# Two cross attentions with keys in rows: four heads at a time in the quarters of TensorE's array, and the maxima as one more row of the product

## The chip, the cores and the metric

The kernel runs on one core of a Trainium2 chip. The metric is the device time of one execution in microseconds (us). Each time shown is one execution; the median of the runs is compared.

## What is computed

The program is a decoder of four blocks, each with a self attention, a cross attention and a feed-forward part (twelve sub-layers), on x of 2 x 1024 tokens with 256 features. After each sub-layer comes `x = layernorm(x + sublayer(x))`. The change concerns the cross attentions of the first two blocks. Their keys are a context of 2 x 154 rows with 192 features; there are 16 heads of 16 features. Cut to what matters:

```
q = (x @ wq + bq)   k = (ctx @ wk + bk)   v = (ctx @ wv + bv)      # heads: 16 x 16
scores = einsum('bhqd,bhkd->bhqk', q, k) / sqrt(16)
scores = clip(scores, -10000, 10000)        # second block only
attn = softmax(scores, axis=-1)
out = einsum('bhqk,bhkd->bhqd', attn, v).reshape(B, Sq, 256) @ wo + bo
```

## The kernel before

`run` (L2473) calls the twelve sub-layers in the order of `LAYERS` (L2470). `l0_xattn` (L624) and `l1_xattn` (L627, with a limit of 40000 on the unscaled scores) both call `xattn` (L637). The 2048 tokens lie as 16 tiles of 128 (`x`, tokens in the partitions). Around it stand `post_norm` (L320), which normalises all 16 tiles after the sub-layer before, and the loads of the next sub-layer's weights (`after_loads`).

`xattn` first calls `xattn_keys`: it makes the keys with features in the partitions and lays them out eight times with all heads but one masked (`kx`, on GpSimd, `masked_heads` L631), makes V with keys in the partitions, writes it to DRAM and reads it back so that the 16 x 154 pairs of head and key lie one after the other in 20 chunks of 128 rows (`vb`, L2058 to L2071). Then `start_features` (L298) transposes x, two 128x128 transposes a tile, and `features` (L308) makes the queries. All products are f32. On the page one f32 product is two MATMUL instructions, one transpose is one.

The loop over the 16 tiles has these steps for each tile:

- six products with 128 rows of contraction, two or three masked heads each (L661, 462 or 308 columns, into `pa`);
- for each of them a maximum over the keys (L667, VectorE) and a subtraction (L668, VectorE in the first of the two layers, GpSimd in the second); in the second layer a clip before it (L665, VectorE);
- two exponentials of 128x1232 (L670, ScalarE);
- 20 transposes of 128x128 (L677), and five copies out of PSUM that ScalarE (L237) and VectorE (L239) take in turn;
- 20 products of the chunks with V (L689), whose last column of each head sums the weights;
- `attend_out` (L703): the reciprocal (L697) and the division (L699), two transposes (L286), the product with wo and one with a row of ones for the bias (L244), the residual (L312) and the statistics of the norm (L353, L354).

PSUM has eight banks of 128x512 f32: four of `pa`, two of `pt`, two of `po`. No order of work is written out: each engine takes its instructions in the order in which a scheduler put them at build time, and that lets the transposes and the products of one tile stand between the products of the next.

Of the kernel before, what the change touches and what calls it, by code (L numbers as in the profile page):

```python
# [25 lines left out]
T = B * S  # L26
# [16 lines left out]
def _columns():  # L43
# [7 lines left out]
    for l in ("L0", "L1", "L2"):  # L51
        v += [(f"{l}_xattn_bq", D), (f"{l}_xattn_bk", D)]
# [19 lines left out]
def _offsets(items, width):  # L72
    off, n = {}, 0
    for name, length in items:
# [9 lines left out]
          ("later", 32), ("upto", 32), ("hmask", 8), ("desc", 8), ("slots", CAP), ("rel", 17), ("eps", 2), ("vmask", 2 * NCH), ("tok", NT), ("blk", 2 * NT + NE - 1),  # L84
# [4 lines left out]
def _constants():  # L89
# [21 lines left out]
        "vmask": vmask,  # L111
        "cos": by_tile(cos), "sin": by_tile(sin),
# [12 lines left out]
def _layout(inputs):  # L125
# [3 lines left out]
    g["L3_xattn_kn_g"] = np.tile(g["L3_xattn_kn_g"], 2)  # L129
    cols = np.zeros((128, NCOL), np.float32)  # L130
# [20 lines left out]
    for m in "qkvo":  # L151
        a[f"L0x_w{m}"] = g[f"L0_xattn_w{m}"]
        a[f"L1x_w{m}"] = g[f"L1_xattn_W{m}"]
# [30 lines left out]
class Decoder:  # L184
# [426 lines left out]
    def load_xattn(self, pre, layer):  # L611
        s = self.slot()
        w = {m: self.load(s, self.ins[f"{pre}_w{m}"], 96 if m in "kv" else 128) for m in "qkvo"}
        w["bv"] = self.rows(s, f"{layer}_xattn_bv", D)
        w["bo"] = self.rows(s, f"{layer}_xattn_bo", D)
        return w
# [20 lines left out]
    def xattn(self, w, after_loads, layer, clip):  # L637
        nc, tc = self.nc, self.tc
        after_loads()
        chunks = self.xattn_chunks()  # L640
        with ExitStack() as cx:
            dram = cx.enter_context(tc.tile_pool(name="xadram", bufs=1, space=bass.MemoryType.DRAM))
            p1 = cx.enter_context(tc.tile_pool(name="xa1", bufs=1))
            p = cx.enter_context(tc.tile_pool(name="xa", bufs=2))
            kx, vb = self.xattn_keys(w, layer, p1, p, dram)
            self.start_features()
            vz = p1.tile([128, B, H, HD + 1], F, name="vz")
            nc.gpsimd.memset(vz, 0.0)
            for b in range(B):
                nc.gpsimd.tensor_copy(vz[:, b, 0:chunks[0][1]], vb[:, b, 0, 0:chunks[0][1]])  # L650
            qT = p1.tile([128, 2, T], F, name="qT")
            self.features(qT, w["q"], AF.Identity, f"{layer}_xattn_bq")
            for i in range(NT):
                b = i // TPB
                e = p.tile([128, H, SK], F, name="e")
                mx = p.tile([128, H], F, name="mx")
                for c in range(2):
                    for h0, n in ((0, 3), (3, 3), (6, 2)):
                        ps = self.pa()
                        s3 = ps[:, :n * SK].rearrange("p (h k) -> p h k", h=n)  # L660
                        nc.tensor.matmul(s3, qT[:, c, i * 128:(i + 1) * 128], kx[:, b, c, h0:h0 + n], start=True, stop=True)  # L661
                        g = slice(c * 8 + h0, c * 8 + h0 + n)
                        sub = nc.vector
                        if clip is not None:
                            nc.vector.tensor_scalar(e[:, g], s3, clip, -clip, ALU.min, ALU.max)  # L665
                            s3, sub = e[:, g], nc.gpsimd
                        nc.vector.tensor_reduce(mx[:, g], s3, AX.X, ALU.max)  # L667
                        sub.tensor_tensor(e[:, g], s3, mx[:, g].unsqueeze(2).to_broadcast([128, n, SK]), ALU.subtract)  # L668
                    g = slice(c * 8, c * 8 + 8)
                    nc.scalar.activation(e[:, g], e[:, g], AF.Exp, scale=0.25)  # L670
                eT = p.tile([128, NCH, 128], F, name="eT")
                flat = e.rearrange("p h k -> p (h k)")
                for k0 in range(0, NCH, 4):
                    ps = self.pt()
                    for k in range(k0, k0 + 4):
                        r = chunks[k][2]
                        nc.tensor.transpose(ps[:r, (k - k0) * 128:(k - k0 + 1) * 128], flat[:, k * 128:k * 128 + r], self.ident)  # L677
                    n = 4 if chunks[k0 + 3][2] == 128 else 3
                    self.copy(eT[:, k0:k0 + n].rearrange("p k t -> p (k t)"), ps[:, :n * 128])
                    if n == 3:  # L680
                        r = chunks[k0 + 3][2]
                        nc.vector.tensor_copy(eT[:r, k0 + 3], ps[:r, 384:512])
                av = self.po()
                for k, (h0, n, r) in enumerate(chunks):
                    if k == 0:
                        dst, src = av[:, :H * 17], vz[:, b].rearrange("p h d -> p (h d)")
                    else:
                        dst, src = av[:, h0 * 17:(h0 + n) * 17], vb[:r, b, k, 0:n].rearrange("p a d -> p (a d)")
                    nc.tensor.matmul(dst, eT[:r, k], src, start=(k == 0), stop=(k == NCH - 1))  # L689
                self.attend_out(p, i, av, w["o"], w["bo"])  # L690
# [1340 lines left out]
    def xattn_chunks(self):  # L2031

# [7 lines left out]
    def xattn_keys(self, w, layer, p1, p, dram):  # L2040
# [7 lines left out]
        for b in range(B):  # L2048
# [16 lines left out]
            for c in range(2):  # L2065
                self.masked_heads(kx[:, b, c], kT[:, c, b * SK:(b + 1) * SK], SK)
# [450 lines left out]
```

## Time and profile before

| what | value |
|---|---|
| runs | 3918.94, 3889.13, 3898.75 us; median 3898.75 us |
| profiled execution | 3905.38 us, its span 3903.6 us |
| mean granted TensorE clock | 0.902 |
| first cross attention: norm begins, first score product, last statistics | 780.4, 812.1, 1032.4 us |
| second: norm begins, first score product, last statistics | 1909.1, 1933.9, 2174.5 us |

Times are read from the span's start. PE is TensorE's products and PEld its loading of weights, which runs beside them; DVE is VectorE, ACT ScalarE, POOL GpSimd. "PEclk" is the granted clock of TensorE as a share of full speed. A line of groups gives the source line, the engine, the tile written and the tiles read, their shapes, the count, the busy time and the mean of one in ns, and the idle time of that engine just before them with what ended it. For a product, "32\*128 32x512" reads: 32 rows of contraction, 128 columns of weights, 512 columns that move through. A line of windows gives the busy time (and count) of each engine in one stretch of the span, the granted clock, and what the DMA engines did.

### The profile page before, as it was taken

The numbers are of one execution on the slowest core, as the hardware profiler recorded it, in microseconds if no ns is written. First come the engines' busy times: TensorE is split into PE (matmuls) and PEld (weight loads), VectorE is DVE, ScalarE is ACT, GpSimd is POOL, SyncE is SP. The second block draws the span as 40 slices with busy tenths as digits, with TensorE's granted clock in tenths as the row PEclk, the third lists the DMA queues.
The fourth block names the chain that finished last, engine by engine and source line by source line (L and its number), as shares of the span: only waits on it lengthen the run. The fifth ranks groups of instructions, "written<-read, shape, count | busy, mean of one in ns | idle before, by whom it ended". The sixth has DMA issues, their size and how long they took to land. (4 is left out here: it accounts for less than half of the span.)

```text
span 3903.6 us, 55156 instructions
## 1 busy us (share of the span) xinstructions
PE 3382.5 (87%) x22758; PEld 2236.2 (57%) x22776; DVE 1906.1 (49%) x3855; ACT 1166.2 (30%) x2063; POOL 577.2 (15%) x674
## 2 busy tenths in 40 slices
PE   8997999899779996599999479999979477789988
PEld 3544666567669995488677245544557233443345
DVE  2466765366621116787566766400020434557741
ACT  3542345333201114322222452311112233332221
POOL 0000000010023322200233113100022432210000
PEclk9996789899779998799999689999979799899989
DMA  2235432000168882466300000300023100000000
GB/s 92 74 84 136 100 77 76 7 7 1 43 242 314 324 318 72 160 272 266 95 1 1 7 8 1 120 0 0 23 94 124 62 1 25 1 1 1 1 1 22
DMA packets 181525, 317.49 MB, mean 81 GB/s; under 512 B 68176, under 2 KB 153242, under 8 KB 172186
## 3 DMA queue, kind: packets, MB, share of 16 engines
q1 hardware_dynamic: 169866, 191.13, 15.4%
q0 software_dynamic: 11408, 122.83, 8.1%
q8 instruction: 180, 2.95, 0.3%
q14 instruction: 71, 0.58, 0.0%
HBM read 265.63 MB, written 48.28 MB: 80 GB/s over the span
## 5 line engine op out<-in xcount | busy, mean ns | idle before, releaser
L244 PEld LDWEIGHTS pa<-xgT,ew 128*128 128x128 f32 x2184 | 251.4, 193 | 2.8 <-DVE xgT L816 0.8
L244 PE MATMUL pa<-xgT,ew 128*128 128x128 f32 x2184 | 251.7, 276 | 0.4 <-DVE xgT L816 0.4
L244 PE MATMUL pa<-xT,w 128*128 128x512 f32 (+3 forms) x480 | 228.1, 618 | 0.7 <-DVE xT L239 0.7
L244 PE MATMUL pa<-ha,w 128*128 128x512 f32 x512 | 220.4, 592 | 0.0
L834 DVE TENSOR_TENSOR hid<-a,pa 128x512 f32<-128x512 f32 x78 | 48.5, 621 | 294.2 <-ACT a L833 254.1
L661 PE MATMUL pa<-kx,qT 128*128 128x462 f32 (+1 forms) x384 | 174.8, 573 | 0.9 <-DVE e L668 0.5
L244 PEld LDWEIGHTS pa<-ha,w 128*128 128x128 f32 x512 | 97.3, 190 | 122.5 <-issue 122.5
L960 PE MATMUL pa<-win_k,cst 128*128 128x272 f32 x512 | 128.7, 402 | 43.5 <-DVE win_k L957 43.5
L689 PEld LDWEIGHTS po<-vb,eT 128*128 128x128 f32 (+1 forms) x1216 | 154.8, 197 | 20.3 <-issue 15.1
L689 PE MATMUL po<-vb,eT 128*128 128x34 f32 (+2 forms) x1216 | 151.9, 274 | 0.0
L237 ACT COPY eT<-pt 128x512 f32<-128x512 f32 (+2 forms) x127 | 67.5, 531 | 276.9 <-PE pt L677 221.5
L2455 DVE COPY lg<-po 128x8 f32<-128x8 f32 x16 | 2.7, 167 | 301.9 <-PE po L2452 301.9
L286 PE MATMUL pt<-cst,x 128*128 128x128 f32 x288 | 60.6, 317 | 99.4 <-DVE x L320 66.1
L244 PE MATMUL po<-w,h 128*128 128x256 f32 (+1 forms) x640 | 144.4, 382 | 0.0
L244 PEld LDWEIGHTS pa<-xT,w 128*128 128x128 f32 (+2 forms) x480 | 85.5, 189 | 98.5 <-issue 92.4
L960 PEld LDWEIGHTS pa<-win_k,cst 128*128 128x128 f32 x512 | 98.7, 195 | 63.4 <-issue 38.5
L244 PEld LDWEIGHTS po<-w,h 128*128 128x128 f32 (+1 forms) x640 | 113.2, 179 | 30.6 <-issue 8.5
L244 PE MATMUL po<-ew,hid 128*128 128x256 f32 x546 | 125.3, 379 | 0.0
L986 PE MATMUL po<-win_v,cst 128*128 128x256 f32 x544 | 120.0, 379 | 0.0
L244 PE MATMUL pa<-w,xT 128*128 128x256 f32 (+2 forms) x640 | 102.7, 323 | 15.1 <-ACT sq L1535 3.5
L833 ACT ACTIVATE a<-pa 128x512 f32<-128x512 f32 x78 | 42.4, 544 | 241.7 <-PE pa L244 241.7
L286 PEld LDWEIGHTS pt<-cst,x 128*128 128x128 f32 x288 | 38.6, 159 | 129.1 <-issue 49.9
(557 smaller groups left out, 7074.9 us busy)
## 6 DMA issues: line engine op xcount, KB each, us to landing
win_k<-kd SPq DMA_DIRECT2D x16, 2176.0 KB
win_v<-vd SPq DMA_DIRECT2D x16, 2176.0 KB
w<-in_L2f_eW_dram SPq DMA_DIRECT2D x16, 1024.0 KB
pk<-pk SPq DMA_DIRECT2D x96, 128.0 KB
rw<-pk SPq DMA_DIRECT2D x64, 128.0 KB
y<-yd SPq DMA_DIRECT2D x16, 512.0 KB
ld<-lgs SPq DMA_DIRECT2D x64, 64.0 KB
li<-ld SPq DMA_DIRECT2D x16, 256.0 KB
```

Source lines behind the costliest of these rows:

```text
L237: self.nc.scalar.copy(dst, src)
L244: self.nc.tensor.matmul(out, l, r, start=(i == 0), stop=(i == n - 1))
L286: self.nc.tensor.transpose(ps[:, c * 128:(c + 1) * 128], src[:, c * 128:(c + 1) * 128], self.ident)
L661: nc.tensor.matmul(s3, qT[:, c, i * 128:(i + 1) * 128], kx[:, b, c, h0:h0 + n], start=True, stop=True)
L689: nc.tensor.matmul(dst, eT[:r, k], src, start=(k == 0), stop=(k == NCH - 1))
L833: nc.scalar.activation(a[:, :n], pa[:, :n], AF.Silu)
L834: nc.vector.tensor_tensor(hid[:, m0:m1_].rearrange("p m t -> p (m t)"), a[:, :n], pg[:, :n], ALU.mult)
L960: nc.tensor.matmul(ps[:, 0:W * H], self.ident, win[:, :, d * H:(d + 1) * H], start=(d == 0), stop=(d == HD - 1))
L986: nc.tensor.matmul(ps[:, 0:D], self.ident, win[:, k], start=(k == 0), stop=(k == W - 1))
L2455: self.nc.vector.tensor_copy(lg[:, g * 4 + k], ps[:, :NE])
```

## The change

Both layers get a new loop; nothing else of the program is changed but the layout of their weights.

- **Layout.** On the host the query and key weights and biases are padded so that each head takes 32 feature rows: 16 with data, 16 with zeros (`wide`). Queries and keys have 512 rows, four groups G of four heads, each head in one quarter of the array's rows. Row 16 of each head holds 1 in the keys (`kb`) and a shift in the queries. V has 32 columns a head, the upper 16 of them ones, which sum the weights.
- **Scores with keys in rows.** For four tiles (512 tokens) at once, a group of four heads and 77 keys, four products in the four quarters give 77x512 scores each, in two double banks of PSUM (L737). Two exponentials of 77x1024 read them (and in the second layer two clips on VectorE follow). The products with V take the exponentials as they lie, in the four quarters of the columns (L815), so the 20 transposes a tile, their copies and V's way through DRAM fall away.
- **Maxima.** The maxima over keys are found beforehand from products with tokens in rows: eight jobs for four tiles (`find_maxima`, L710), each of eight quarter products of 154 columns into two double banks, and two reductions of 128x616. They are negated (`negate`), transposed (`shift`, four transposes) and added to the queries, where they become row 16.
- **The rest of a tile** is `divide` (four transposes, reciprocal, division), `features` (four transposes for two tiles, a copy) and `output` (two products of two passes each for a tile, residual and statistics). The output bias is added to x on GpSimd.
- **Order.** There are four groups g of four tiles. Eight steps a group are written out, and TensorE's instructions keep that order (`in_order`): the score products of the next step, one job of maxima for the group after, one piece of the group before (`pieces`), the products with V, the copy (odd steps) or the shift of the next four heads (even steps), a second job in steps 0, 3 and 6, and one piece of `prepare` for the group after the next. Group 0's queries and maxima come ahead of the loop, the last group's pieces behind it.
- **PSUM.** `wide_banks` makes one `pa`, three double banks `wide` and one `po`. Scores and jobs take turns in the three double banks; in the loop every small step (a piece, a shift, a piece of prepare) goes through the one `pa`. Ahead of the loop these steps rotate over `pa` and the double banks (`any_bank`).

The diff, with the removed body of the loop (printed above) and of `xattn_keys` left out:

```diff
-    for l in ("L0", "L1", "L2"):
-        v += [(f"{l}_xattn_bq", D), (f"{l}_xattn_bk", D)]
+    for l in ("L0", "L1"):
+        v += [(f"{l}_xattn_bq", 2 * D), (f"{l}_xattn_bk", 2 * D)]
+    v += [("L2_xattn_bq", D), ("L2_xattn_bk", D)]
...
+        "extra": p % 32 == HD,
...
+    wide = lambda t: np.pad(t.reshape(*t.shape[:-1], H, HD), [(0, 0)] * t.ndim + [(0, HD)]).reshape(*t.shape[:-1], 2 * D)
+    for l in ("L0", "L1"):
+        for m in "qk":
+            g[f"{l}_xattn_b{m}"] = wide(g[f"{l}_xattn_b{m}"])
...
-        a[f"L0x_w{m}"] = g[f"L0_xattn_w{m}"]
-        a[f"L1x_w{m}"] = g[f"L1_xattn_W{m}"]
+        as_is = wide if m in "qk" else (lambda t: t)
+        a[f"L0x_w{m}"] = as_is(g[f"L0_xattn_w{m}"])
+        a[f"L1x_w{m}"] = as_is(g[f"L1_xattn_W{m}"])
...
-        w["bo"] = self.rows(s, f"{layer}_xattn_bo", D)
+        w["bo"] = self.rows_all(s, f"{layer}_xattn_bo", D)
...
     def xattn(self, w, after_loads, layer, clip):
         nc, tc = self.nc, self.tc
         after_loads()
+        self.wide_banks()
+        since = len(nc.cur_bb.bb.instructions)
         with ExitStack() as cx:
             p1 = cx.enter_context(tc.tile_pool(name="xa1", bufs=1))
             p = cx.enter_context(tc.tile_pool(name="xa", bufs=2))
+            kp = p1.tile([128, 4, B * SK], F, name="kp")
+            vp = p1.tile([KH, B, 2, H, 2 * HD], F, name="vp")
+            pad = p1.tile([128, 4, 4, 4, 2 * HD], F, name="pad")
+            kb = p1.tile([128, 4], F, name="kb")
+            nc.gpsimd.memset(vp, 1.0)
+            nc.gpsimd.memset(pad, 0.0)
+            o = COLS[f"{layer}_xattn_bk"]
+            nc.vector.tensor_tensor(kb, self.cols[:, o:o + 4], self.k("extra").to_broadcast([128, 4]), ALU.add)
+            self.bank = self.any_bank
+            for G in range(4):
+                ps = self.bank()
+                self.mm(ps[:, :B * SK], [(w["k"][:96, c, G * 128:G * 128 + 128], self.ctxT[:96, c]) for c in range(2)])
+                nc.scalar.activation(kp[:, G], ps[:, :B * SK], AF.Identity, bias=kb[:, G:G + 1])
+            groups = NT // 4
+            fed = self.fed
+            tiles, maxima, ready = {}, {}, {}
+            def turned(src):
+                ps = self.bank()
+                for c in range(2):
+                    for t in range(2):
+                        nc.tensor.transpose(ps[:, c * 256 + t * 128:c * 256 + t * 128 + 128], src[:, t, c * 128:c * 128 + 128], self.ident)
+                return ps.rearrange("p (c t) -> p c t", c=2)
+            def prepare(g):
+                for t in range(g * 4, g * 4 + 4, 2):
+                    if not fed:
+                        self.copy(self.xT[:, :, t * 128:t * 128 + 256], turned(self.x[:, t:t + 2]))
+                        yield True
+                    for i in (t, t + 1):
+                        nc.gpsimd.tensor_tensor(self.x[:, i], self.x[:, i], w["bo"], ALU.add)
+                q = tiles[g] = p.tile([128, 4, 512], F, name="q", bufs=3)
+                for G in range(4):
+                    ps = self.bank()
+                    self.mm(ps, [(w["q"][:, c, G * 128:G * 128 + 128], self.xT[:, c, g * 512:g * 512 + 512]) for c in range(2)])
+                    nc.scalar.activation(q[:, G], ps, AF.Identity, bias=self.col(f"{layer}_xattn_bq", G))
+                    yield True
+            def find_maxima(g):
+                m = maxima[g] = p.tile([128, 4, 4, 4], F, name="m16")
+                b = g * 4 // TPB
+                for t in range(4):
+                    for G0 in range(0, 4, 2):
+                        pair = [self.wide() for _ in range(2)]
+                        for G in (G0, G0 + 1):
+                            for j in range(4):
+                                R = slice(32 * j, 32 * j + 32)
+                                o = j % 2 * 512 + (G - G0) * SK
+                                nc.tensor.matmul(pair[j // 2][:, o:o + SK], tiles[g][R, G, t * 128:t * 128 + 128],
+                                                 kp[R, G, b * SK:b * SK + SK], start=True, stop=True)
+                        for k in range(2):
+                            s = pair[k].rearrange("p (j n) -> p j n", j=2)[:, :, 0:2 * SK].rearrange("p j (G k) -> p j G k", G=2)
+                            nc.vector.tensor_reduce(m[:, t, 2 * k:2 * k + 2, G0:G0 + 2], s, AX.X, ALU.max)
+                        yield True
+            def negate(g):
+                m = maxima.pop(g)
+                if clip is not None:
+                    nc.vector.tensor_scalar(m, m, clip, 240.0 - clip, ALU.min, ALU.max)
+                for j in range(4):
+                    nc.vector.tensor_scalar(pad[:, :, :, j, HD], m[:, :, j], -1.0, None, ALU.mult)
+            def shift(g, G):
+                ps = self.bank()
+                for t in range(4):
+                    nc.tensor.transpose(ps[:, t * 128:t * 128 + 128], pad[:, t, G].rearrange("p j d -> p (j d)"), self.ident)
+                nc.vector.tensor_tensor(tiles[g][:, G], tiles[g][:, G], ps, ALU.add)
+            def scores(g, G, n):
+                b = g * 4 // TPB
+                pair = [self.wide() for _ in range(2)]
+                o = b * SK + n * KH
+                for j in range(4):
+                    R = slice(32 * j, 32 * j + 32)
+                    nc.tensor.matmul(pair[j // 2][:KH, j % 2 * 512:j % 2 * 512 + 512], kp[R, G, o:o + KH], tiles[g][R, G],
+                                     start=True, stop=True)
+                e = p.tile([KH, 4, 512], F, name="e", bufs=3)
+                for k in range(2):
+                    s = e[:, 2 * k:2 * k + 2].rearrange("p j q -> p (j q)")
+                    nc.scalar.activation(s, pair[k][:KH], AF.Exp, scale=0.25)
+                    if clip is not None:
+                        nc.vector.tensor_scalar(s, s, 1.0, float(np.exp(-60.0)), ALU.min, ALU.max)
+                return e
+            def divide(i, av, t):
+                ps = self.bank()
+                for G in range(4):
+                    nc.tensor.transpose(ps[:, G * 128:G * 128 + 128], av[:, G, t * 128:t * 128 + 128], self.ident)
+                a = ps.rearrange("p (h d) -> p h d", h=H)
+                rs = p.tile([128, H], F, name="rsum")
+                nc.vector.reciprocal(rs, a[:, :, HD])
+                if t % 2 == 0:
+                    ready[i // 2] = p.tile([128, 2, D], F, name="o")
+                nc.vector.tensor_tensor(ready[i // 2][:, t % 2].rearrange("p (h d) -> p h d", h=H), a[:, :, 0:HD],
+                                        rs.unsqueeze(2).to_broadcast([128, H, HD]), ALU.mult)
+            def features(k):
+                oT = p.tile([128, 2, 256], F, name="oT")
+                self.copy(oT, turned(ready.pop(k)))
+                ready[k] = oT
+            def output(k):
+                oT = ready.pop(k)
+                ps = self.bank()
+                for t in range(2):
+                    self.mm(ps[:, t * 256:t * 256 + 256], [(oT[:, c, t * 128:t * 128 + 128], w["o"][:, c]) for c in range(2)])
+                for t in range(2):
+                    self.residual(2 * k + t, ps[:, t * 256:t * 256 + 256])
+            def pieces(g, av):
+                i = g * 4
+                d = [lambda t=t: divide(i + t, av, t) for t in range(4)]
+                f = [lambda k=i // 2 + k: features(k) for k in range(2)]
+                u = [lambda k=i // 2 + k: output(k) for k in range(2)]
+                return [d[0], d[1], d[2], f[0], d[3], u[0], f[1], u[1]]
+            first = prepare(0)
             for b in range(B):
+                for n in range(2):
+                    next(first, None)
+                    o = b * SK + n * KH
+                    ps = self.bank()
+                    self.mm(ps[:KH, :D], [(self.ctxT[:96, c, o:o + KH], w["v"][:96, c]) for c in range(2)] + [self.row_pair(w["bv"], KH)])
+                    self.copy(vp[:, b, n, :, 0:HD], ps[:KH, :D].rearrange("p (h d) -> p h d", h=H))
+            for _ in first:
+                pass
+            ahead = prepare(1)
+            for _ in find_maxima(0):
+                next(ahead, None)
+            for _ in ahead:
+                pass
+            negate(0)
+            shift(0, 0)
+            self.bank = self.pa
+            e = scores(0, 0, 0)
+            behind = []
+            for g in range(groups):
+                b = g * 4 // TPB
+                ahead = prepare(g + 2) if g + 2 < groups else iter(())
+                jobs = find_maxima(g + 1) if g + 1 < groups else iter(())
+                av = p.tile([128, 4, 512], F, name="avs")
+                for s in range(8):
+                    G, n = divmod(s, 2)
+                    nxt = (g, *divmod(s + 1, 2)) if s < 7 else (g + 1, 0, 0)
+                    en = scores(*nxt) if nxt[0] < groups else None
+                    if s < 6:
+                        next(jobs, None)
+                    if behind:
+                        behind.pop(0)()
+                    if n == 0:
+                        ps = self.po()
+                    for j in range(4):
+                        nc.tensor.matmul(ps[32 * j:32 * j + 32], vp[:, b, n, 4 * G + j], e[:, j], start=(n == 0), stop=(n == 1))
+                    if n:
+                        nc.scalar.copy(av[:, G], ps)
+                    elif G < 3:
+                        shift(g, G + 1)
+                    if s % 3 == 0:
+                        next(jobs, None)
+                    next(ahead, None)
+                    if g + 1 < groups:
+                        if s == 5:
+                            for _ in jobs:
+                                pass
+                            negate(g + 1)
+                        if s == 6:
+                            shift(g + 1, 0)
+                    e = en
+                for f in behind:
+                    f()
+                behind = pieces(g, av)
+            for f in behind:
+                f()
+            self.in_order(since)
+        self.psum(4, 2, 2)
...
+    def wide_banks(self):
+
+        self.psum_close()
+        cx = self.psum_cx = ExitStack()
+        PS = bass.MemoryType.PSUM
+        self.psa, self.psx, self.pso = [cx.enter_context(self.tc.tile_pool(name=n, bufs=b, space=PS))
+                                        for n, b in (("psa", 1), ("psx", 3), ("pso", 1))]
+        self.pst = None
+        self.turn_bank = 0
+
+    def any_bank(self):
+
+        self.turn_bank = (self.turn_bank + 1) % 4
+        return self.wide()[:, 0:512] if self.turn_bank else self.pa()
```

## The prediction

> **What bounds the kernel now.** I read the shares of the page, then the granted clock and busy times by stage (windows), then the waits in the first layer's loop, then the products that already use parts of the array (timeline). First the page:
>
> ```profile
> PE 3382.5 (87%) x22758; PEld 2236.2 (57%) x22776; DVE 1906.1 (49%) x3855; ACT 1166.2 (30%) x2063; POOL 577.2 (15%) x674
> ...
> L661 PE MATMUL pa<-kx,qT 128*128 128x462 f32 (+1 forms) x384 | 174.8, 573 | 0.9 <-DVE e L668 0.5
> ...
> L689 PE MATMUL po<-vb,eT 128*128 128x34 f32 (+2 forms) x1216 | 151.9, 274 | 0.0
> ```
>
> The second column from the right is the idle time before: PE waits 0.9 us before 384 score products and never before 1216 products with V. By stage (length, then busy PE, PEld, DVE, ACT, POOL, granted clock, DMA):
>
> ```profile
> 779.00:812.00 33.00, 29.17 (x95) 14.95 (x96) 17.80 (x30) 9.65 (x20) 12.64 (x11) 0.90 0.20 21
> 812.00:1024.00 212.00, 210.86 (x1259) 162.44 (x1257) 148.13 (x330) 67.24 (x83) 0.00 (x0) 0.98 0.00 1
> 1024.00:1033.00 9.00, 5.85 (x25) 3.78 (x24) 2.42 (x8) 0.50 (x2) 0.00 (x0) 0.62 0.06 14
> 1905.00:1934.00 29.00, 25.45 (x83) 12.78 (x82) 10.73 (x31) 10.18 (x20) 3.33 (x8) 0.88 0.52 118
> 1934.00:2164.00 230.00, 228.29 (x1272) 172.82 (x1270) 149.26 (x330) 67.17 (x83) 83.03 (x96) 0.91 0.00 1
> 2164.00:2175.00 11.00, 5.52 (x15) 3.39 (x14) 7.12 (x13) 0.31 (x1) 0.00 (x0) 0.50 0.06 15
> 3090.00:3310.00 220.00, 163.76 (x933) 74.92 (x943) 88.88 (x257) 72.33 (x150) 73.85 (x58) 0.94 0.00 1
> 3540.00:3730.00 190.00, 179.46 (x870) 63.86 (x870) 137.87 (x168) 61.77 (x64) 0.00 (x0) 0.99 0.00 1
> ```
>
> Each layer is a start (33, 29 us), a loop (212, 230) with PE over 99% busy, and an end (9, 11). So PE's work sets the loop. The second loop is longer at the same work because its clock is 0.91. The last two rows are block 3's attentions, at a clock of 0.94 and 0.99 although PE is busy 74% and 94%. The waits of the first loop agree: everyone waits for PE.
>
> ```profile
> ACT eT L237 <- PE pt L677: 135.7, 46, 7.1
> ...
> DVE rsum L697 <- PE po L689: 17.5, 15, 1.2
> DVE eT L239 <- PE pt L677: 13.4, 30, 0.8
> ```
>
> What a set of four quarter products costs stands in block 3 (start, length):
>
> ```profile
> 3161.12 1.06 PE L1445 MATMUL po<-e,v 128*32 128x512 f32 x8
> 3162.12 1.04 PE L1432 MATMUL pa<-m_own,identb 128*128 128x512 bf16 x4
> 3163.09 1.14 PE L1436 MATMUL pa<-qT,kT 32*128 32x512 f32 x8
> 3164.16 0.44 PE L286 MATMUL pt<-cst,o 128*128 128x128 f32 x2
> ```
>
> Start to start, four column quarters take 1.00 us and four row quarters 1.07; a full product of 512 columns takes 0.86 (two instructions of 0.43). So four run nearly at once.
>
> **The change part by part.** Prices at full clock, from rows: set of row quarters 1.05, of column quarters 1.0, four transposes 0.44 (0.11 each), queries of four heads for four tiles 1.71 (four instructions of 0.43), output of two tiles 1.73 (eight of 0.216); 0.21 from the last pass to the reader's start, and about 0.1 wherever the array changes its division (1.07 against 0.96 of pure passes). Exp 77x1024 1.11 (the L2012 row), copy of 512 columns 0.59 on ACT and 0.69 on DVE, shift add 0.69, reciprocal 0.26, division 0.41, residual with statistics 1.02. A reduction of 616 is not in the trace: 308 took 0.47, 462 took 0.63, 1024 took 1.22; I take 0.78 on that line, bounds 0.63 and 1.22. The clip of 77x1024 in SBUF is bounded by 0.61 (the L1022 tensor_scalar of 2048 elements, 1.22, halved) and 1.22 (the L1611 add of 77x1024); I take 0.64, near the row of its own kind. A job's eight quarter products of 154 columns I take as 0.71 (two 64-row halves of two products took 0.40).
>
> *PE's work falls.* Before, a tile took 212/16 = 13.2 us. Now a group of four tiles takes 8 score sets 8.4, 8 V sets 8.0, 8 jobs 5.7, 48 transposes 5.2, queries 6.8, output 3.5, some 30 changes of division about 3: 40 us, against 53. Without the queries of groups 0 and 1, group 0's jobs, the shifts of its start and the last group's pieces, the loop holds 134 us.
>
> *But the order adds waits.* A typical even step (group 1, step 2, first layer), from its start: scores 0 to 1.05; exps 1.26 to 2.37 and to 3.48. The job's first two products take the third double bank at once; its third needs the first bank of the scores just issued, so it waits for the exp: 1.24 to 2.42, end 2.95. Reductions 3.16 to 3.94 and to 4.72. Divide transposes 2.95 to 3.49, but DVE has the reductions first: its reciprocal and division end at 5.39. V products end at 4.48. The shift needs the only pa bank: waits to 5.44, transposes to 5.98, add 6.19 to 6.88. The piece of prepare waits for pa again: 6.93 to 8.63. So 8.63 us for 5.5 of PE work, with waits of 1.2 (exp), 1.0 (division) and 1.0 (add). In the second layer two clips on DVE stand ahead of the reductions: the division ends 0.97 later, the step takes 9.6. An odd step without a second job (step 1) takes 6.0 and 6.9.
>
> Carried on through all steps: first layer 43.9 + 54.8 + 44.3 + 27.2 + 1 = 171 us at full clock; second 48.8 + 61.8 + 49.8 + 36.8 + 1 = 198. At a clock of 0.95 (between 0.94 and 0.99 above and the 0.91 of this layer before) PE's part stretches: 176 and 201.6. Before 212 and 230: **-36 and -28**.
>
> A page speaks against such a change: the Trainium skill, "TensorEngine Tiling (Array Packing)", section PSUM Bottleneck, says that packing speeds up TensorE but not the reading of PSUM, which may then be the limit. By that alone the loop would go by the busiest reader's sum (DVE in the second layer, about 116 us), below PE's 134, and the layer would gain; the trace's lines speak for waits by order in its place.
>
> *The start grows.* From the last product of the sub-layer before (779.1): keys 4 x 1.04, V 4 x 1.5, two turns of 0.44 and queries 4 x 1.71 = 18; the x copies on DVE wait for post_norm, which ends about 9 us in: 20. Then eight jobs beside the next group's turns and queries, all rotating over three double banks and pa: 20. Negate 0.8, shift 1.5: 42.5, at the clock of 0.90 44.8. First loop product at 823.9 instead of 812.1: **+12**. Second layer: 1905.3 + 44.8 = 1950 instead of 1933.9: **+16**. The way of V through DRAM, the masked copies (9 us on POOL) and the wider weights (loaded a stage earlier) hide in this, before and after. POOL's new memsets (0.55 for 544 elements, so about 2 each) and the additions of bo (0.82 each) lie beside DVE's norm and can slow it by a few us: bounds 0 to +4, I take 0 extra.
>
> *The end grows.* The last group's eight pieces go one after the other through pa: 16.8 us with 6 of PE. The clock fell to 0.62 and 0.50 in the ends before; at 0.6 this is 20.5. Before 8.4 (to 1032.4) and 10.5 (to 2174.5): **+12, +10**. In the second, VectorE's preparation of the next feed-forward's weights (11.8 us, which ran at the end and behind it) comes to stand between the divisions: up to +10 here, -8 behind: **+2**.
>
> The sum: +12 - 36 + 12 = -12; +16 - 28 + 10 + 2 = 0. Together -12 to -13 against the profiled execution (3905.4): 3892.8. That execution lies 6.6 above the median, so the forecast is **3886 us**.
>
> **The rivals.** *Waits shorter (faster).* If the unseen costs are at their low ends (changes of division 0.05, exp 1.02 as in the L2014 row, reduction 0.72, clip 0.61, clock 0.99), the loops take 165 and 189: -11 and -12.5, and the starts and ends together -6: about -30, 3856. For it: all stalls are in chains of such costs. If PE's work alone counted (134/0.95 = 141 us), -35 and -60 on the forecast: about 3790. Against that: the third product of each job cannot pass the exp.
>
> *The clock falls (slower).* The new loop leaves PE idle 1 us several times a step, and in the ends, where PE waited likewise, the clock was 0.62 and 0.50. At 0.75 the loops take 203 and 222 (+48 on the forecast) and starts and ends 15 more: 3949. It ends over 1% slower than before from about 0.78 down. Against it: 0.94 at 74% busy in block 3, and this loop is 78% busy.
>
> *The quarters don't run at once for 77 keys.* Four products in a row cost 3.84 instead of 1.05: 64 sets a layer +179, jobs +90: about 4420. Against it: the 32\*128 and the 128\*32 sets above.
>
> **How the numbers follow.** About 1% (39 us) is what a measurement of this kernel can tell from no change. Forecast 0.50 (its own range 3860 to 3937). Waits shorter 0.25 and PE alone 0.03: faster 0.28. Clock 0.15, quarters 0.02, and 0.05 for reductions at 1.22, clips at 1.22 and slower norms together (loops 192 and 236 at a clock of 0.9, +16 and +34, norms +8, starts and ends +6: about 3950): slower 0.22. The range reaches to the shorter waits and the lower clock and leaves out PE alone and the quarters: 3840 to 3950, with 15 us below the shorter waits because the step that PE need not wait for a bank is the least certain.
>
> **What would show it.** Right: loops of 171 to 180 and 195 to 206 us at PE busy about 78%, PE idle before the jobs' products released by ACT's exp and before shifts and prepare by DVE; starts of about 45, ends of about 20 us. Wrong: idle under 15 us in a loop (waits hidden), a granted clock under 0.85, sets of quarters over 1.3 us, or a maximum's reduction near 1.2.

## The result and the profile after

The change makes no difference that can be measured: 3909.45 us median of 20 runs against 3903.09 us of the kernel before, ratio 1.0006 with a 95% interval of 0.9985 to 1.0027. The forecast of 13 us less (0.9968) lies below that interval. The first layer gained about what was forecast; the second lost it again.

The engines' busy times fell as the change meant them to, on the page of the changed kernel:

```profile
PE 3315.3 (85%) x22774; PEld 2075.9 (53%) x22792; DVE 1814.4 (46%) x3605; ACT 1199.0 (31%) x2083; POOL 498.7 (13%) x580
...
L742 ACT ACTIVATE e<-wide 77x1024 f32<-77x1024 f32 x128 | 123.9, 1018 | 103.2 <-PE wide L737 103.2
...
L714 DVE TENSOR_REDUCE m<-wide 128x4 f32<-128x616 f32 x128 | 96.1, 792 | 87.4 <-PE wide L710 87.3
```

TensorE is busy 67 us less over the program (3382.5 before) and the time is the same. In the two loops below PE is busy 84% and 83% of the time, over 99% before, so its work alone no longer sets them. The same stages as before, from the start of the norm ahead of a layer to the first loop product, to the end of the last product with V, to the norm behind the layer (length, busy times, and the granted clock as the third number from the right):

```profile
781.43:821.70 40.27, 36.16 (x217) 19.17 (x216) 22.09 (x41) 10.92 (x17) 7.25 (x9) 0.92 0.00 1
821.70:999.10 177.40, 149.60 (x1125) 67.36 (x1125) 67.30 (x137) 78.54 (x92) 5.63 (x8) 0.94 0.00 1
999.10:1020.70 21.60, 12.94 (x44) 8.43 (x40) 7.66 (x27) 2.77 (x4) 0.00 (x0) 0.60 0.05 16
1895.12:1933.70 38.58, 34.04 (x219) 17.93 (x217) 22.35 (x42) 10.66 (x17) 6.54 (x8) 0.97 0.18 63
1933.70:2144.40 210.70, 175.26 (x1125) 78.51 (x1126) 108.87 (x204) 78.76 (x92) 5.63 (x8) 0.81 0.00 1
2144.40:2172.34 27.94, 13.50 (x44) 9.14 (x44) 18.90 (x40) 2.77 (x4) 0.00 (x0) 0.63 0.04 13
```

Read the clock: 0.94 in the first loop, 0.81 in the second. PE runs the same 1125 instructions in both, in 149.6 us and in 175.3. The stage of the first layer takes 239.3 us (252.7 before), that of the second 277.2 (269.0 before).

Why do they differ? One step with a shift and a job, first in the first layer, then in the second (start, length, and in brackets PE's idle time and who ended it):

```profile
871.57 1.32 PE L737 MATMUL wide<-q,kp 32*77 32x512 f32 x8
872.72 0.53 PE L710 MATMUL wide<-kp,q 32*128 32x154 f32 x4
874.12 0.79 PE L710 MATMUL wide<-kp,q 32*128 32x154 f32 x12 [0.86 <-ACT e L742]
874.84 0.66 PE L750 MATMUL pa<-cst,avs 128*128 128x128 f32 x4
875.43 1.07 PE L815 MATMUL po<-e,vp 77*32 77x512 f32 x8
877.00 0.63 PE L728 MATMUL pa<-cst,pad 128*128 128x128 f32 x4 [0.51 <-DVE o L756]
```

```profile
2027.67 1.10 PE L737 MATMUL wide<-q,kp 32*77 32x512 f32 x8
2028.59 0.43 PE L710 MATMUL wide<-kp,q 32*128 32x154 f32 x4
2029.88 0.79 PE L710 MATMUL wide<-kp,q 32*128 32x154 f32 x12 [0.86 <-ACT e L742]
2030.60 0.66 PE L750 MATMUL pa<-cst,avs 128*128 128x128 f32 x4
2031.18 1.06 PE L815 MATMUL po<-e,vp 77*32 77x512 f32 x8
2033.64 0.63 PE L728 MATMUL pa<-cst,pad 128*128 128x128 f32 x4 [1.39 <-DVE o L756]
2035.05 1.98 PE L252 MATMUL pa<-xT,w 128*128 128x512 f32 x4 [0.78 <-DVE q L729]
```

From its third product on the job waits 0.86 us for the exponential in both (1.2 in the prediction). The shift waits for the division 0.51 us in the first layer and 1.39 in the second (the prediction had 1.0 and 0.97 more), because VectorE has two clips (L744) ahead of the reductions and the division:

```profile
2029.86 0.69 DVE L744 TENSOR_SCALAR e<-e 77x1024 f32<-77x1024 f32 x1 [2.51 <-ACT e L742]
2030.77 0.69 DVE L744 TENSOR_SCALAR e<-e 77x1024 f32<-77x1024 f32 x1 [0.22 <-ACT e L742]
2031.38 1.49 DVE L714 TENSOR_REDUCE m<-wide 128x4 f32<-128x616 f32 x2
2032.79 0.24 DVE L753 RECIPROCAL rsum<-pa 128x16 f32<-128x16 f32 x1
2033.07 0.42 DVE L756 TENSOR_TENSOR o<-pa,rsum 128x256 f32<-128x256 f32 x1
```

So far this was in the step table. The clock was not. In the records it is at full or at half speed, in stretches of 3.41 us or multiples of it. Here are three and two neighbouring 3.41-us windows of the second loop of the changed kernel, cut on that grid (the second number is PE's busy time of the 3.41):

```profile
2044.31:2047.72 3.41, 3.41 (x23) 0.99 (x21) 0.14 (x2) 1.82 (x3) 0.00 (x0) 1.00 0.00 0
2047.72:2051.14 3.42, 1.79 (x16) 0.65 (x12) 2.50 (x4) 0.80 (x1) 0.00 (x0) 1.00 0.00 0
2051.14:2054.55 3.41, 3.41 (x11) 2.31 (x8) 1.38 (x2) 1.93 (x2) 0.00 (x0) 0.50 0.00 0
...
2071.62:2075.03 3.41, 1.49 (x12) 0.42 (x4) 2.56 (x6) 0.00 (x0) 0.00 (x0) 1.00 0.00 0
2075.03:2078.44 3.41, 2.50 (x12) 1.11 (x12) 0.19 (x1) 1.04 (x2) 0.00 (x0) 0.50 0.00 0
```

and of its first loop:

```profile
846.23:849.65 3.42, 2.50 (x32) 1.18 (x30) 0.69 (x1) 2.58 (x3) 0.00 (x0) 1.00 0.00 0
849.65:853.06 3.41, 3.41 (x32) 1.48 (x28) 2.32 (x4) 0.82 (x2) 0.00 (x0) 1.00 0.02 5
853.06:856.47 3.41, 2.49 (x32) 1.10 (x24) 0.88 (x2) 2.38 (x3) 0.00 (x0) 1.00 0.00 0
```

A window with PE busy 1.79 us (52%) or 1.49 (44%) is followed by one at half clock; the first loop's windows with 2.5 us (73%) are not. The first loop's waits mostly leave 73% or more; the second's, a little longer and close together, now and then leave half.

### The profile page after: what moved, and what is told of

Its sections match the earlier page's. It is cut to its first block, busy times and chain, and to the rows that moved or that the text cites. A ratio compares the mean times of both kernels' runs of the same rounds, so it can differ in the third digit from the quotient of the medians.

```text
span 3908.0 us, 54809 instructions
## 1 busy us (share of the span) xinstructions
PE 3315.3 (85%) x22774; PEld 2075.9 (53%) x22792; DVE 1814.4 (46%) x3605; ACT 1199.0 (31%) x2083; POOL 498.7 (13%) x580
## 3 DMA queue, kind: packets, MB, share of 16 engines
q1 hardware_dynamic: 150222, 191.05, 14.5%
## 4 chain that ended last, share of the span: by engine, by line
PE 70%; DVE 16%; ACT 5%; POOL 4%; issue 2%; DMA 2%; SPq 0%; POOLq 0%; DVEq 0%; ACTq 0%
PE pa L252 27%; PE po L252 9%; PE pa L1107 3%; PE wide L737 2%; PE po L1753 2%; PE wide L2156 2%; DVE win_v L1127 2%; PE pa L1443 1%; POOL n L1552 1%; PE wide L252 1%; PE wide L2121 1%; PE pt L294 1%; ACT e L742 1%; PE po L815 1%; PE wide L710 1%
## 5 line engine op out<-in xcount | busy, mean ns | idle before, releaser
L252 PE MATMUL pa<-xT,w 128*128 128x512 f32 (+3 forms) x488 | 237.6, 629 | 8.8 <-DVE q L729 7.5
L742 ACT ACTIVATE e<-wide 77x1024 f32<-77x1024 f32 x128 | 123.9, 1018 | 103.2 <-PE wide L737 103.2
L714 DVE TENSOR_REDUCE m<-wide 128x4 f32<-128x616 f32 x128 | 96.1, 792 | 87.4 <-PE wide L710 87.3
L294 PE MATMUL pt<-cst,x 128*128 128x128 f32 x224 | 48.7, 320 | 89.9 <-DVE x L328 65.0
L1133 PEld LDWEIGHTS po<-win_v,cst 128*128 128x128 f32 x544 | 103.4, 190 | 14.5
L252 PEld LDWEIGHTS po<-ew,hid 128*128 128x128 f32 x546 | 100.2, 190 | 11.8
L2161 ACT ACTIVATE e<-wide 128x1024 f32<-128x1024 f32 x64 | 65.6, 1025 | 129.4 <-PE wide L2156 128.7
```

Of the source, the lines that this page charges most:

```text
L252: self.nc.tensor.matmul(out, l, r, start=(i == 0), stop=(i == n - 1))
L294: self.nc.tensor.transpose(ps[:, c * 128:(c + 1) * 128], src[:, c * 128:(c + 1) * 128], self.ident)
L714: nc.vector.tensor_reduce(m[:, t, 2 * k:2 * k + 2, G0:G0 + 2], s, AX.X, ALU.max)
L742: nc.scalar.activation(s, pair[k][:KH], AF.Exp, scale=0.25)
L1133: nc.tensor.matmul(ps[:, 0:D], self.ident, win[:, k], start=(k == 0), stop=(k == W - 1))
L2161: nc.scalar.activation(e, wide, AF.Exp)
```

## The experiments

The theory under test: the clips' place on VectorE lengthens single waits of PE in the second layer until a 3.41-us window falls to about half busy, and then the clock halves. Rivals: the clock belongs to that one run; it comes from what runs before the second layer; it comes from the clips' work as such, wherever it stands. Two more edits ask what the one pa bank costs, in the loop and at the end.

Every profile gave these stages (us, granted clock of the loop in brackets):

| kernel | first: start, loop, end | second: start, loop, end |
|---|---|---|
| before | 32.1, 213.5 (0.98), 7.1 | 24.8, 230.6 (0.91), 13.6 |
| e1 before again | 32.1, 213.5 (0.98), 7.1 | 24.8, 221.1 (0.95), 13.6 |
| changed | 40.3, 177.4 (0.94), 21.6 | 38.6, 210.7 (0.81), 27.9 |
| e2 changed again | 41.9, 181.5 (0.90), 21.6 | 38.6, 214.7 (0.80), 29.1 |
| e3 only first | 42.0, 177.1 (0.94), 20.2 | 24.6, 220.5 (0.95), 13.6 |
| e4 only second | 33.3, 212.0 (0.99), 7.1 | 38.5, 214.7 (0.80), 29.2 |
| e5 no clip | 42.0, 177.2 (0.94), 20.2 | 38.6, 177.1 (0.94), 29.1 |
| e6 clip in first too | 38.1, 210.7 (0.80), 21.6 | 38.4, 209.1 (0.82), 29.2 |
| e7 late clip | 42.0, 177.1 (0.94), 20.3 | 38.5, 214.6 (0.80), 29.1 |
| e8 tail banks | 38.1, 176.8 (0.94), 12.4 | 38.5, 214.5 (0.80), 18.6 |
| e9 late clip, order kept | 42.0, 173.8 (0.97), 22.9 | 38.5, 189.9 (0.91), 29.6 |
| e10 piece first | 38.1, 163.3 (0.96), 21.7 | 38.6, 184.2 (0.90), 29.2 |
| e11 all three | 38.1, 163.8 (0.96), 13.5 | 38.6, 177.1 (0.95), 24.4 |
| e12 order kept in loop | 39.8, 160.0 (0.99), 12.4 | 38.6, 180.1 (0.93), 18.8 |

**e1 and e2, both kernels once more (no edit).**

> The kernel before, unchanged, for a second profile: how far stages that nobody changed move from one profile to another. If the clock of a stage is a matter of the run (rival), its second loop, 230 us at a granted clock of 0.91, and block 3's attention (window of 220 us at 0.94) differ by 5 us or more and by 0.03 or more of clock. If the clock belongs to the kernel (theory), both stay within 3 us and 0.02.

> The changed kernel, unchanged, for a second profile. Theory: the second layer's loop is long because TensorE's granted clock is low in it whenever this code runs: again 207 to 214 us at 0.79 to 0.84, the first layer's loop 174 to 181 us at 0.92 to 0.96. Rival (the clock was that run's): the second loop 198 to 204 us at 0.90 or more.

The old second loop in the first profile and in e1, then the new one in e2:

```profile
1933.90:2164.50 230.60, 228.89 (x1273) 173.34 (x1271) 149.26 (x330) 67.17 (x83) 83.03 (x96) 0.91 0.00 1
...
1918.10:2139.20 221.10, 219.38 (x1273) 168.01 (x1271) 148.82 (x330) 67.08 (x83) 83.03 (x96) 0.95 0.00 1
...
1936.50:2151.20 214.70, 177.72 (x1125) 78.77 (x1126) 108.91 (x204) 78.94 (x92) 5.63 (x8) 0.80 0.00 1
```

e1 and e2 are one execution each (3889.58 and 3915.96 us). The clock of the new second loop came again: 0.80, 214.7 us, just past the expected 214, and e4, e7 and e8 have it at 0.80 once more; so it belongs to the kernel. The new first loop took 181.5 us at 0.90, outside what was expected; it holds one half-clock stretch of 23.9 us that no other first loop without clips has. The old second loop moved from 230.6 us at 0.91 to 221.1 at 0.95 between two profiles, and block 3's attention by 4 us. So the run's rival holds for the old loop and falls for the new second one, and the 230 us that the prediction started from is the longest of three samples (e3 shows 220.5 once more).

**e3 and e4, one layer alone.** Edit: the other layer calls the old `xattn` with the old weights.

```diff
-        self.xattn(w, after_loads, "L1", 40000.0)
+        self.xattn_old(w, after_loads, "L1", 40000.0)     # e3; e4 the same for L0
```

> Only the first layer's cross attention is the new one, the second is as before. Theory: the first layer gains 13 us (from the start of the norm ahead of it to the norm behind it 239 instead of 253 us) and the time falls by about that, ratio 0.9967. Rival (the gain of the first layer is lost again in later stages by a lower clock): the stage gains 13 us and the time stays, ratio 0.999 to 1.001.

> Only the second layer's cross attention is the new one. Theory: its stage takes 275 to 279 us instead of 265, and the time rises by 8 to 16 us, ratio 1.002 to 1.004, with a granted clock of 0.79 to 0.84 in its loop although the first layer's old loop came before. Rival (the low clock in the second layer comes from the new first layer): loop 198 to 204 us, clock 0.9 or more, ratio 0.999 to 1.001.

e3: ratio 0.9979 (0.9952 to 1.0007), stage 239.3 instead of 252.7 us. e4: 1.0005 (0.9977 to 1.0033), stage 282.4 us with the loop at 0.80 although the old first layer ran before it. The intervals are too wide to tell 0.998 from 1; the stages are clear, though e4's is 3 us longer than the 275 to 279 expected. The new first layer is not what brings the second's clock down.

**e5, the clips left out, and e6, the clips in the first layer too.**

```diff
-                    if clip is not None:                       # e5: removed
-                        nc.vector.tensor_scalar(s, s, 1.0, float(np.exp(-60.0)), ALU.min, ALU.max)
+                    if True:                                   # e6: in both layers
+                        nc.vector.tensor_scalar(s, s, 1.0, float(np.exp(-60.0)), ALU.min, ALU.max)
```

> The changed kernel without the two clips of 77x1024 a step in the second layer (the limits of its exponentials are left out of the computation). The second loop is then the first layer's loop. Theory (the clips, ahead of the reductions and the division on VectorE, make single waits of TensorE so long that the granted clock drops): second loop 174 to 184 us at a clock of 0.90 or more, from 211 to 215 at 0.80. Of that 27 us are the waits at full clock, the rest the clock. Rival (the clock in the second layer is low because of what runs before it): clock still 0.79 to 0.84, loop 190 to 196.

> The changed kernel with the same two clips in the first layer as well (its exponentials are limited to between exp(-60) and 1, which they nearly keep anyhow). Theory: the first loop becomes like the second, 205 to 216 us at a clock of 0.78 to 0.86, from 177 to 182 at 0.90 to 0.94. Rival (the place in the program sets the clock): 198 to 203 us at 0.92 or more.

Both as the theory had it (e6 is a single execution, 3929.65 us). Without the clips the second loop is the first one, and with them the first is the second one; windows of the two loops of e5, then of e6:

```profile
809.70:986.90 177.20, 149.14 (x1125) 67.58 (x1126) 67.34 (x137) 78.30 (x92) 5.63 (x8) 0.94 0.00 1
...
1922.40:2099.50 177.10, 149.14 (x1125) 67.52 (x1126) 68.28 (x140) 78.31 (x92) 5.62 (x8) 0.94 0.00 1
```

```profile
811.50:1022.20 210.70, 176.52 (x1125) 77.98 (x1126) 107.88 (x201) 78.87 (x92) 5.62 (x8) 0.80 0.00 1
...
1956.60:2165.70 209.10, 172.88 (x1125) 76.64 (x1125) 108.70 (x204) 78.74 (x92) 5.62 (x8) 0.82 0.00 1
```

The clips add 41 us of VectorE work and 33 to 38 us to a loop of 177 us, and with them VectorE is busy only half of it. Of these 33 to 38 us, 6 to 9 are more idle time of PE (27 to 28 us without clips, 34 to 37 with them); in the rest PE's same 1125 instructions take longer (149 to 155 us without, 173 to 178 with them). e5 takes 1% less than the kernel before, 0.9901 (0.9866 to 0.9936), but it leaves the limits out.

**e7 and e9, the clips behind the reductions and the division.** e7 takes the two clips out of `scores` and issues them later; e9 also keeps VectorE's program order, as `in_order` does for PE.

```diff
+            def limit(e):
+                if clip is not None:
+                    for k in range(2):
...
                     if behind:
                         behind.pop(0)()
+                    if en is not None:
+                        limit(en)
...
             self.in_order(since)
+            self.in_order(since, mybir.EngineType.DVE)         # e9 only
```

> The clips are issued after the step's job and piece, ahead of the products with V, so that reductions and division stand before them on VectorE. The same work. Theory: second loop 188 to 194 us at a clock of 0.88 or more (186.6 at full clock by the step table), about 20 us less than with the clips ahead, ratio 0.993 to 0.998. Rival (the clock stays near 0.81): 201 to 206 us.

> As the late clip, but VectorE's instructions in the two layers now keep the program's order too, so that the clips do stand behind the job's reductions and the division. The same work, no product moved. Theory (it is the place of the clips, which makes single waits of TensorE longer, that brings the clock down): second loop 188 to 194 us at 0.88 or more; first loop 175 to 182 as before; ratio 0.993 to 0.998. Rival (the clips' work on VectorE as such, wherever it stands): 201 to 216 us at 0.79 to 0.84.

e7 is a miss: 214.6 us at 0.80, ratio 1.0035 (1.0004 to 1.0065), and in its trace the clips, reductions and reciprocals stand in the same order on VectorE as in the changed kernel, the clips ahead:

```profile
1978.85 0.69 DVE L749 TENSOR_SCALAR e<-e 77x1024 f32<-77x1024 f32 x1 [0.22 <-ACT e L742]
1979.46 1.49 DVE L714 TENSOR_REDUCE m<-wide 128x4 f32<-128x616 f32 x2
1980.87 0.24 DVE L757 RECIPROCAL rsum<-pa 128x16 f32<-128x16 f32 x1
```

VectorE's order is the scheduler's, and PE's kept order does not bind it. With the order kept (e9) the same work takes 189.9 us at 0.91, within the expected 188 to 194; ratio 0.9959 (0.9930 to 0.9989). A step of e9's second loop:

```profile
2006.96 0.79 PE L710 MATMUL wide<-kp,q 32*128 32x154 f32 x12 [0.86 <-ACT e L742]
2007.69 0.66 PE L754 MATMUL pa<-cst,avs 128*128 128x128 f32 x4
2008.28 1.07 PE L822 MATMUL po<-e,vp 77*32 77x512 f32 x8
2009.85 0.63 PE L728 MATMUL pa<-cst,pad 128*128 128x128 f32 x4 [0.51 <-DVE o L760]
```

The shift's wait is back at 0.51 us, the first layer's. So it is mostly the clips' place, not their work: the kept order takes back 25 of the 38 us, 4 of them as idle time of PE (36.8 us in e7, 32.8 in e9) and the rest through the clock. The edit keeps all of VectorE's order, in both layers, and the first loop, which has no clips, also fell by 3 us (173.8, expected 175 to 182); so some 3 of the 25 may not be the clips'.

**e8, the last group's pieces over all banks, and e10, the piece ahead of the job.**

```diff
+            self.bank = self.any_bank                          # e8
             for f in behind:
                 f()
...
-                    if s < 6:                                  # e10
-                        next(jobs, None)
                     if behind:
                         behind.pop(0)()
+                    if s < 6:
+                        next(jobs, None)
```

> The last group's eight pieces rotate over pa and the three double banks, as the steps ahead of the loop do, in place of the one pa. Theory (the ends are a chain through one bank): ends from 21 to 14 us in the first layer and from 28 to 20 in the second; loops unchanged. Rival (the ends are set by the low clock and by the weight preparation on VectorE): ends within 2 us of before.

> In each step the piece of the group before is issued ahead of the job of maxima, in both layers; the clips stay where they are. The transposes of a division then run while the exponentials do, and the shift finds the pa bank free earlier. Theory (the waits for the one pa bank behind division and reductions are what the loop's order costs; by the step table 158 us at full clock instead of 171 in the first layer, 190 instead of 198 in the second): first loop 160 to 168 us at 0.93 or more, second 193 to 206 us. Rival (the waits only move to the third product of the job, which then waits longer for the exponential): first loop within 4 us of 177.

e8: ends of 12.4 and 18.6 us instead of 21 and 29, loops unchanged; 0.9978 (0.9950 to 1.0007). The first end's clock rose from 0.60 to 1.00 as PE's idle time in it fell from 8.7 to 5.1 us. e10: loops of 163.3 and 184.2 us, better than expected in the second; PE's idle time in it went from 36.7 us (e8) to 24.6 and its clock from 0.80 to 0.90. The clips' place in the program is unchanged, but in the trace 8 of the 12 divisions in the loop now stand between the two clips and ahead of the reductions (from 1981.79 us: clip, reciprocal, division, clip, reductions), so this run changes their order on VectorE too. Ratio 0.9905 (0.9868 to 0.9943).

**e11 and e12, all three edits together.** e12 keeps VectorE's order only up to the end of the loop.

```diff
+            self.in_order(since, mybir.EngineType.DVE)         # e12: here
             self.bank = self.any_bank
             for f in behind:
                 f()
             self.in_order(since)
-            self.in_order(since, mybir.EngineType.DVE)         # e11: here
```

> Piece ahead of the job, clips behind reductions and division with VectorE's order kept, and the last group's pieces over all banks. Theory: first loop 160 to 168 us, second 180 to 190 us at a clock of 0.9 or more, ends 12 and 15 to 19 us; about 14 + 9 in the first layer and 25 + 10 in the second below the changed kernel, ratio to the kernel before 0.983 to 0.989. Rival (what is saved in waits lowers the clock elsewhere or is taken by other waits): ratio 0.992 or more.

> As the one with all three edits, but VectorE's order is kept in the loop only and not in the last group's pieces, where the weight preparation of the next sub-layer may stand elsewhere. Theory: loops as there (164 and 177 us), the second end 18 to 20 us instead of 24, the first 12 to 13; another 5 us, ratio to the kernel before 0.982 to 0.988. Rival (the second end is set by the preparation's own 12 us on VectorE, wherever it stands): second end 23 us or more, ratio as there.

e11: 0.9875 (0.9833 to 0.9917); its second end was 24.4 us where e8 had 18.6. With the order released there (e12) it is 18.8, so the kept order was the cause and not the 12 us of weight preparation as such. e12: 3844.02 us median against 3897.23, ratio 0.9850 (0.9815 to 0.9884): 1.5% below the kernel before, which the changed kernel equals (1.0006). Its two loops:

```profile
827.70:987.70 160.00, 143.40 (x1125) 61.98 (x1126) 69.27 (x136) 78.19 (x92) 5.63 (x8) 0.99 0.00 1
...
1915.40:2095.50 180.10, 153.37 (x1125) 64.90 (x1126) 107.89 (x203) 78.48 (x92) 6.97 (x8) 0.93 0.00 1
```

## Why the prediction was wrong

The terms of its sum, against the two profiles of each kernel:

| term | forecast | measured |
|---|---|---|
| first start | +12 | +8 and +10 |
| first loop | -36 | -36 and -32 |
| first end | +12 | +14.5 |
| second start | +16 | +14 |
| second loop | -28 | -20 and -6 |
| second end, with the weight preparation behind | +12 | +11 to +12 |

The last measured row is 14.3 to 15.5 us more in the stage, and about 3.6 less in the stage behind it (893.1 us on average from norm to norm with the old second layer in three profiles, 889.5 with the new one in three).

*Right.* PE's work fell and stopped being the limit; the waits were the ones named (exponential before a job's third product, division before the shift, add before the piece of prepare). The first layer came out at -13 and -8 us where -12 was forecast, partly by luck: the table has 134 us of PE work and 37 of waits in the first loop, and the trace, with busy time at half clock counted half, 139 and 28; the clock took another 10, where the sum had 5. The unseen prices held: the reduction of 616 took 0.79 us (0.78 taken), the clip 0.69 (0.64), the exponential 1.02 (1.11). Quarters of 77 keys ran at once: a set of scores took 1.10.

*Wrong: above all one term, the second loop.* The step that failed is "At a clock of 0.95 ... PE's part stretches: 176 and 201.6". One clock was taken for both loops, from block 3's attentions and the old loop, though the step worked out just ahead of it waits 0.97 us longer in the second. Measured were 0.94 and 0.90 in the first, 0.81 and 0.80 in the second, and a loop of 210.7 and 214.7 us: 9 to 13 us over the 201.6. Inside, the miss is larger. The sum gave the second loop 64 us of waits at full clock (198 less 134) and 3.6 for the clock; the traces show 35 to 37 us of PE's idle time, and the low clock stretches about 137 us of work to 175 and 178, by 38 to 41 us. The two partly go together: in the 80 to 87 us at half clock PE is idle only 4 us, in the rest of the loop 32. The same step table at 0.81 gives 215 us, but for that reason it is no proof of the table. Another 9 us come from the starting point: the old loop's 230.6 us was at a clock of 0.91, and two other profiles have 221 at 0.95. Together they are about 20 us, and that is the gap between the forecast's 0 for the second layer and what e2 and e4 show against e1 and e3: a stage of 282.4 us against 259.5 and 258.6, less the 3.6 behind it, +19 to +20.

The slower rival named the right mechanism with the wrong reach: a lower clock in both loops. It needs waits as in the second layer, and e5 and e6 show that these come from the clips, whichever layer has them. The clips cost 33 to 38 us a loop; the table had 27 for them, all as waits at full clock, and the traces show 6 to 9 as waits. The mean of 0.94 at 74% busy in block 3, which the prediction held against this rival, could not speak for the second loop: it does not say how evenly the waits lie.

*Later stages.* The sum has nothing for the stages behind but the 8 us of weight preparation. Block 3's attention, in code that nobody changed, took 249.2 to 250.0 us at 0.87 in eight of the ten profiles with both layers new and 257.0 and 257.2 at 0.84 in the other two (e10, e11); with an old layer in the program it took 242.3 to 246.3 at 0.89 to 0.91 (four profiles). Before and changed:

```profile
3069.50:3311.80 242.30, 177.49 (x987) 83.74 (x1000) 102.51 (x301) 78.03 (x163) 85.41 (x69) 0.91 0.01 1
3062.90:3312.60 249.70, 186.73 (x987) 88.95 (x1000) 102.85 (x301) 78.26 (x163) 86.91 (x69) 0.87 0.01 1
```

So 3 to 8 us are lost there by the clock, and more in e10 and e11.

*Open.* Why block 3's clock falls is not shown; ten profiles against four make chance unlikely. Half-clock stretches last 3.41 us mostly, but some in these loops last 24 to 41 us while PE is busy 73 to 100% of each window, and no run tells what ends them. They hold 41 to 51 of the 80 to 87 us at half clock in the second loop as it was changed; e5, e9, e10, e11 and e12 have none. So the runs show that the clips' place brings the low clock, but only part of it is traced window by window.

## What to carry to other kernels

When a change takes the limit off PE and leaves it waiting, price the waits twice: as lost time, and by whether any 3.41-us stretch falls to about half busy, since in these loops the work after it mostly ran at half speed. Here the second price was the larger. Work on an engine that is half idle can still cost nearly its full length if it stands ahead of what PE waits for, and a kept order on one engine does not order the others: look in the trace at the engine that answers. A base read from one profile is a sample; a second one is worth having where a stage's clock is below 1.

## What the runs showed of the hardware

The granted clock is full or half, in steps of 3.41 us. Take the 22 loops of the new kind in these profiles, cut on that grid: of the 54 full-clock windows with PE busy less than 55%, 45 were followed by one at half clock; of the 77 between 55 and 65%, 33; of the 777 at 65% or more, 6. The Trainium skill, "TensorE: Matmul & The Clock Gate", Part 1, has the two states and a free-running window of 3413 ns, which agrees. It lets the clock fall after an idle window of about 3.4 us, and also tells of a kernel whose clock swung because PE idled briefly but often. The measurement is on the second side: no single wait of PE in these 22 loops was over 1.9 us, and windows in which it worked half the time were mostly enough.

Busy time is not the whole rule. In the six loops of the old kind PE was busy 99% or more in 330 full-clock windows, and 16 of these were followed by one at half clock. Eleven of the 16 are among the 13 windows in which the short products with V (L689, 17 or 34 columns) filled about 80% or more: in the kernel before, the window from 2043.23 us has PE busy 3.42 of 3.42 us, 88% of it with such products, and the next window is at 0.50. So the old second loop's 0.91 and 0.95 came with hardly any waits (1.7 us of PE's idle time in the loop); why some such windows count and others do not was not tried.

The time from the program's start to the first of these norms, all of it ahead of the first cross attention, which no kernel here changes, went from 764.6 to 803.4 us over the 14 profiles. That scatter is three times the effect that was to be found, which is why the stages, and not the medians, carry the account.
